# Local attention and whitening on one core: VectorE's order in image 0 written out, evictions and the first softmax put first

## The chip, the cores and the metric

The kernel runs on one core of a Trainium2 chip. Five engines work side by side, each through its own queue of instructions in order: TensorE (PE in the profile, its weight loads PEld), VectorE (DVE), ScalarE (ACT), GpSimd (POOL) and SyncE (SP), which issues most of the DMA transfers. Instructions of different engines wait for each other by semaphores. The metric is the device time of one execution in microseconds. Before the change the median of three runs was 827.57 us (821.6 to 827.88).

## What is computed

The input x has 4 images of 256 channels and 64 by 64 pixels. Layer 0 computes 49 attention logits for each pixel by a 7 by 7 convolution with dilation 2 to 128 channels and a 1 by 1 convolution to 49; a softmax over the 49; and the sum of the 49 shifted copies of x with these weights. Layer 1 whitens groups of 64 channels: mean and covariance over all images and pixels, five Newton steps for the inverse square root, and a linear map of every pixel.

```python
k = conv(x, w1, padding=6, dilation=2) + b1      # 128 channels
k = conv1x1(k, w2) + b2                          # 49 channels
attn = softmax(k, axis=1)
y = einsum('bkchw,bkhw->bchw', shifts_of_x, attn)
# layer 1: groups of 64 channels, all pixels of all images
Sigma = EPS * I + cov(y);  P = I
for _ in range(5):
    P = 1.5 * P - 0.5 * P @ P @ P @ (Sigma / trace)
out = (P * sqrt(1 / trace)) @ (y - mean) * weight + bias
```

## The kernel before

**Weights.** The two convolutions have no nonlinearity between them, so the kernel first multiplies the filters (lines 204 to 235): the result is the tile `tap`, 49 logits for each of 7 by 7 taps and 256 channels. `cv_buf` is a pair of PSUM tiles used here first and by the convolution later.

**The convolution by interpolation.** Logits are computed as in a Winograd scheme: polynomials in the row direction and in the column direction are evaluated at 7 points (0, 1, -1, 2, -2, a sixth point and infinity; `EVAL`, `INF`), multiplied, and interpolated back. For one row point `br` this takes: `row_weights` (line 307, sums of taps, into `gbr` or `gb5`, with scratch in `lgx`), `weights` (line 342, the column sums for a bank of column points, into the tiles `wr`, one buffer for each of the three banks), `row_eval` (line 412, sums of the image's rows, into `rb`), `col_eval` (line 443, sums of columns, into the tiles `xh`), `conv_bank` (line 471, the matmuls, into one of the two `cv_buf` tiles, and an eviction by ScalarE into `pv`), and `col_interp` (line 544, 22 small VectorE operations, into `zz`). A row point has three banks of column points, `BANKS`, of 96, 80 and 32 matmuls. VectorE does all sums; it is the busiest engine after TensorE. For each operation of this kind the helper `in_turn` (line 266) can tie the order: while `strict` is set, each such operation is made to follow the one before it.

**Image 0 is different.** Only three of its row points (1, 2, 3) go through the banks. The others (0, 4, 5 and infinity) are computed by `direct` (line 582): 56 matmuls over 7 column taps each, straight from the rows. `direct0` (line 670) lets them write the PSUM tile `acc`, which has two halves; infinity takes the second half, row 0 the first and, later, the second. The result goes to `zz` or `zi` by a ScalarE eviction (line 607), or (line 609 and the next) by a small ScalarE copy and a VectorE addition. `keep_weights` scales the weights of rows 4 and 5 and stores them to DRAM for the images after. Then `row_interp` interpolates over the row points, in two parts, and writes the logits `lg`, for image 0 in the memory of `store[4]`; ScalarE adds the bias (line 578).

**Softmax and weighted sum.** `softmax(b, pc)` (line 742) transposes the logits of one column parity on TensorE into two of the three `tp` buffers, takes the maxima (`mx`) on VectorE, 16 exponentials on ScalarE (`d`), and normalises on VectorE. `move_terms` (line 785) copies the weights with ScalarE into `zt` in skewed form, 16 copies for each of four quarters `n` of an image, and stores `zt` to DRAM (`sd`). `load_band` loads it back shifted, and VectorE transposes it in place (line 852); then the tile `band` is a banded matrix. `make_block` turns pixels by TensorE and evicts them to `xb`; `weighted_sum` multiplies `xb` with `band` into `y`; `store_y` evicts it over the memory of x; `turn_y` turns y again, evicts to `yt`, and `moments` adds to the covariance. The end of the kernel whitens.

**What sets the order.** TensorE's matmuls keep the order of the program (`keep_in_program_order`). On the other engines a scheduler chooses among the ready instructions by priority, so VectorE's and ScalarE's orders come from it, apart from what `in_turn` ties. The loop at line 1079 runs the rows of images 1 to 3 bank by bank, each step with a cost, and spreads over them (`gap`, `todo`) the softmax and the eight half-steps of the image before: `plan` gives each piece one of eight places in an image. In image 1 the direct convolution for infinity (`direct_inf`) follows the first row's three banks; the two softmaxes of image 0 stand at places 0 and 1.

These lines show how the first two direct convolutions stand ahead of the conv steps, and how infinity shares the tile:

```python
direct(0, br, sr, acc[:, 1 if br == INF else sr], w)
...
direct0(INF, 0)
direct0(0, 0)
for k in range(NR0):
    ...
    for i in range(len(BANKS)):
        conv_step(k, i)
```

Of the kernel before, what the change touches and what calls it, by code (L numbers as in the profile page):

```python
# [2 lines left out]

# [20 lines left out]
INF = 6  # L24
# [7 lines left out]
def kernel(  # L32
# [246 lines left out]

    @contextmanager  # L280
    def in_order():
        strict[0] = True
        yield
        strict[0] = False

    def add(o, a, b):
        return in_turn(TT(o, a, b, ALU.add))  # L287
# [54 lines left out]
    def weights(b, br, i):  # L342
# [15 lines left out]
        if br == 0:  # L358
            g = [gr0[:, v] for v in range(KS)]
        elif br in kept:  # L360

            f = rb[0].rearrange("p q r c w -> p (q r c w)")[:, : KS * NSK]
            if i == 0:
                nc.sync.dma_start(f, kept[br])
            f = f.rearrange("p (v a r k) -> p v a r k", v=KS, a=NCC, r=2)
            g = [f[:, v] for v in range(KS)]
        else:
            if i == 0:
                row_weights(br)
            g = [gbr[:, v] for v in range(KS)]  # L370
        g = [t.rearrange("p a r k -> p (a r k)") for t in g]
        e, o, e1 = (
# [98 lines left out]
    def conv_bank(b, br, i, w):  # L471

        if i == 0:
            pvs[b, br] = apool.tile(
                [P, NP, Q9, 2 * Q9], F32, tag="pv", name=f"pv_{b}_{br}", bufs=2
            )
        pts = BANKS[i]
        i0 = sum(len(k) for k in BANKS[:i])
        cv = cv_buf[ncv[0] % 2][:, : 3 * PT].rearrange(
            "p (n q b two) -> p n q b two", n=3, two=2, b=Q9  # L480
        )
        ncv[0] += 1
        for k, bc in enumerate(pts):
            terms = [(sr, sc, cc) for sc in taps(bc) for sr in taps(br) for cc in range(NCC)]
            wv = w[bc].rearrange("p c (a r k) -> p c r a k", r=len(taps(br)), a=NCC)
            for j, (sr, sc, cc) in enumerate(terms):

                n = Q9 if j == 0 and bc == INF else Q8
                for h in range(2):
                    pe(  # L490
                        nc.tensor.matmul(  # L491
                            cv[h * HB : h * HB + KT, k, sr : sr + n, sc : sc + n],
                            wv[:, sc, sr, cc],
                            xh[bc][:, :n, h * NCC + cc, :n],
                            start=(j == 0),
                            stop=(j == len(terms) - 1),
                            skip_group_check=True,
                        )
                    )
        nc.scalar.copy(  # L500
            pvs[b, br][:K2, i0 : i0 + len(pts)].rearrange("p n q b -> p (n q b)"),
            cv[:K2, : len(pts)].rearrange("p n q b two -> p (n q b two)"),
        )

    def interpolate(pt, tmp, outs, cut, part=None):

# [75 lines left out]
    def direct(b, br, s, ps, w, xr=None):  # L582
# [21 lines left out]
                )  # L604
        z = zi[b % 2][:K2] if br == INF else zz[:K2, br]
        if s == 0:
            nc.scalar.copy(z[:, :Q8], ps[:K2])  # L607
        else:
            nc.scalar.copy(z[:, Q8], ps[:K2, Q8 - 1])
            add(z[:, 1:Q8], z[:, 1:Q8], ps[:K2, : Q8 - 1])  # L610

    gi = dram.tile([P, KS, NCC * KT], F32, name="gi")
    nc.sync.dma_start(gi, tap[:, UPOS[3]].rearrange("p v a k -> p v (a k)"))

    def direct_inf(b):

        t = apool.tile([P, KS, NCC, KT], F32, tag="wi", name=f"wi_{b}")
        nc.sync.dma_start(t.rearrange("p v a k -> p (v a k)"), gi.rearrange("p v k -> p (v k)"))
        w = [t[:, v] for v in range(KS)]
        ps = cv_buf[ncv[0] % 2].rearrange("p (q w) -> p q w", w=W)  # L620
        ncv[0] += 1
        direct(b, INF, 0, ps, w)

    acc = ps_y.tile([P, 2, Q8, W], F32, tag="y", name="acc")
    nc.vector.memset(acc, 0.0)
# [11 lines left out]
        nxt.update(w)  # L637
        col_eval(cur["x"], i)

    for i in range(len(BANKS)):  # L640
        prepare(0, i)

    def conv_step(k, i):
        w = {bc: nxt.pop(bc) for bc in BANKS[i]}
        b, br = rows[k]
# [2 lines left out]
        if end:  # L648

            with in_order():  # L650
                if i == len(BANKS) - 2:
                    col_interp(b, br, 0)
                elif i == len(BANKS) - 1:
                    col_interp(b, br, 1)
                    row_interp(b, 1)
        if k + 1 < len(rows) and k != NR0 - 1:
            prepare(k + 1, i)
        if i == len(BANKS) - 1 and not end:
            if b > 0 and br == ROWS[-2]:
# [10 lines left out]
    def direct0(br, sr):  # L670
# [3 lines left out]
        else:  # L674
            u = KS - 1 - 4 * sr - (3 if br == INF else 0)
            w = [tap[:, UPOS[u], v] for v in range(KS)]
            direct(0, br, sr, acc[:, 1 if br == INF else sr], w)

    direct0(INF, 0)
    direct0(0, 0)  # L680
    for k in range(NR0):
        if k == NR0 - 1:
            row_weights(4)
            keep_weights(4)
            xrs[4] = row_eval(0, 4)
        for i in range(len(BANKS)):
            conv_step(k, i)
        if k == 1:
            direct0(0, 1)
            for s in range(2, 4):  # L690
                load_x(s, s, nc.gpsimd)
    row_weights(5)
    keep_weights(5)
    xrs[5] = store[4].rearrange("p c r w -> p (c r w)")[:, SH * W :].rearrange(
        "p (q r c w) -> p q r c w", q=Q8, r=2, c=NCC
    )
    row_eval(0, 5, [rb[0], rb[1], xrs[5]])

    for sr in range(2):
        nc.scalar.copy(  # L700
            gr0[:, :, :, sr].rearrange("p v a k -> p (v a) k"),
            tap[:, UPOS[KS - 1 - 4 * sr]].rearrange("p v a k -> p (v a) k"),
        )
    direct0(4, 0)
    with in_order():
        direct0(4, 1)
        row_interp(0, 0)
    direct0(5, 0)
    for i in range(len(BANKS)):
        prepare(NR0, i)  # L710
    with in_order():
        direct0(5, 1)
        row_interp(0, 1)
    gpool.release()

    npix = SH * W // 4
    nc.vector.tensor_reduce(
        pivot, slots[0].rearrange("p a r w -> p a (r w)")[:, :, :npix], AX.X, ALU.add  # L720
    )
    nc.vector.tensor_scalar(pivot, pivot, -1.0 / npix, None, ALU.mult)

# [61 lines left out]
    def move_terms(n):  # L785
# [7 lines left out]
        for j in range(CR):  # L793
            for u in range(CR):
# [8 lines left out]
                    offset=o[:, e].offset,  # L803
                    ap=[list(o.ap[0]), [KS * SW, NCH], [(KS - CR) * SW, ne], [1, KS]],
                )
                if k % 2 == 0 or b < B - 1:
                    nc.scalar.copy(o, i)  # L807
                else:
                    nc.vector.tensor_copy(o, i)
                k += 1  # L810
        nc.sync.dma_start(
            sd[n % 2].rearrange("(p f) -> p f", p=P),
# [22 lines left out]
    def load_band(n, part):  # L835
# [13 lines left out]
                ),  # L849
            )  # L850
        f = band[:, m0:m1].rearrange("p m r w -> p (m r w)")
        nc.vector.transpose(f, f)  # L852
        if n > 4 * (B - 1):
            bring_back(dma)

# [8 lines left out]
    def make_block(n, m):  # L864
# [9 lines left out]
                )  # L874
            )
        xb = bpool.tile([P, C], F32, tag="xb", name=f"xb_{n}_{m}", bufs=4)
        (nc.vector.tensor_copy if tail else nc.scalar.copy)(xb, t[:, :C])  # L877
        blocks[n, m] = xb


# [27 lines left out]
    def store_y(n, half):  # L908
        yt, pc = where(n)
        ps = y_ps.pop((n, half))  # L910
        for cc in range(NCC):
            o = yt[:, cc, half * HALF : (half + 1) * HALF, bass.ds(pc, SW, 2)]
            if tail and cc:
                nc.vector.tensor_scalar(o, ps[:, cc], pivot[:, cc : cc + 1], None, ALU.add)
            else:
                nc.scalar.activation(o, ps[:, cc], AF.Identity, bias=pivot[:, cc : cc + 1])  # L916

    count = [0]
    ybs = {}
# [1 line left out]
    def turn_y(n, i):  # L921
        yt, pc = where(n)
        t = tp()
        for cc in range(NCC):
# [5 lines left out]
                )  # L930
            )
        yb = ybs[n, i] = yt_buf[i % NY]
        nc.scalar.copy(  # L933
            yb.rearrange("p a g c -> p (a g) c")[:, :, :GW],
            t[:, :C].rearrange("p (e c) -> p e c", c=GW),
        )

    def moments(n, half):

# [108 lines left out]
        todo.setdefault((b + j // NPC, j % NPC), []).extend(what)  # L1048

    def soft(b, pc):  # L1050
        softmax(b, pc)
        soft_done.add((b, pc))
        bands(4 * b + pc)

# [13 lines left out]
            for j in range(8):  # L1068
                plan(b + 1, 3 + j, hs[j])
    for b in range(B):  # L1070
        for j in range(2):
            plan(b + 1, j, lambda b=b, j=j: soft(b, j))
    plan(1, 2, lambda: load_x(4, 4, nc.gpsimd))

# [4 lines left out]
    for b in range(1, B):  # L1079

        steps = []
        for r in range(len(ROWS)):
            k = NR0 + len(ROWS) * (b - 1) + r
            for i, cost in enumerate((6, 5, 2)):
                steps.append((cost, lambda k=k, i=i: conv_step(k, i)))

        steps.insert(len(BANKS) if b == 1 else 0, (12, lambda b=b: direct_inf(b)))
        j, at, whole = 0, 0, sum(c for c, _ in steps)
        for cost, f in steps:
            f()  # L1090
# [169 lines left out]
```

## Time and profile before

The span of the profiled execution is 824.6 us, that of its run 826.37 us.

| stretch, us | PE busy | VectorE busy | ScalarE busy |
|---|---|---|---|
| 0 to 40 | 28.16 | 18.77 | 10.53 |
| 40 to 80 | 27.21 | 40.00 | 7.64 |
| 80 to 120 | 38.86 | 39.93 | 15.01 |
| 120 to 160 | 36.22 | 22.19 | 7.81 |
| 160 to 200 | 39.16 | 38.76 | 12.72 |
| 200 to 220 | 10.81 | 16.80 | 14.95 |
| 220 to 300 | 75.19 | 61.12 | 38.09 |
| 300 to 340 | 36.63 | 38.55 | 16.81 |

Each row is the busy time of an engine in that stretch, so a row is read against its length. Image 0's convolution lies between 33 and 170 us, image 1's begins at 170, the first softmax is at 181 to 215, and the first weighted sum at 216. From 220 on TensorE is busy nearly all the time up to the whitening at 750. The later lines of the profile are read in the same way: start and duration in us, engine and line, what is written from what, and, in brackets, how long the engine sat idle ahead of it and what ended the wait.

### The profile page before, as it was taken

What the parts mean: (1) busy time and instruction counts of PE and PEld (TensorE: products, weight loads), DVE (VectorE), ACT (ScalarE), POOL (GpSimd) and SP (SyncE); (2) the same over time, 40 slices, a digit from 0 to 9 for tenths busy, and PEclk for the clock granted to TensorE, in tenths of its full rate; (3) what the DMA queues carried; (4) which work ended last, traced back from release to release, by engine and by line L of the source; (5) the groups of instructions that cost most, each with busy time, mean ns of one, the idle gap of its engine ahead of it and who ended that gap; (6) DMA issues with size and microseconds to landing.
All of it is one profiled execution on the core that took longest, in us unless ns stands there. A gap on an engine that the chain in (4) does not pass through costs nothing.

```text
span 824.6 us, 18450 instructions
## 1 busy us (share of the span) xinstructions
PE 733.9 (89%) x7444; PEld 550.4 (67%) x7444; DVE 620.4 (75%) x1314; ACT 346.2 (42%) x1018; POOL 34.0 (4%) x46
## 2 busy tenths in 40 slices
PE   5839999899589989988999999889999789888997
PEld 1416762276469877777899948778897668675443
DVE  2799992999697979988986999498979654444443
ACT  1321440126654524468433435665334563322443
POOL 0310000030000010001000100000000000000000
PEclk9979999999789999999999999899999999899999
DMA  8990210043534472066445621442421137810576
GB/s 332 206 315 20 76 70 1 30 150 114 163 118 153 169 236 70 19 221 228 145 120 188 196 57 31 125 169 74 156 66 38 46 118 242 243 46 2 229 305 281
DMA packets 60013, 114.76 MB, mean 139 GB/s; under 512 B 22759, under 2 KB 41880, under 8 KB 59032
## 3 DMA queue, kind: packets, MB, share of 16 engines
q1 hardware_dynamic: 56232, 94.71, 35.3%
q0 software_dynamic: 3696, 18.88, 6.8%
q8 instruction: 59, 0.97, 0.5%
q14 instruction: 26, 0.21, 0.1%
HBM read 66.23 MB, written 47.33 MB: 138 GB/s over the span
## 4 chain that ended last, share of the span: by engine, by line
PE 45%; DVE 31%; ACT 13%; DMA 6%; issue 4%; SPq 0%; DVEq 0%; ACTq 0%
PE y L898 13%; PE cv L491 7%; ACT zt L807 7%; PE tp L1206 7%; PE acc L596 4%; DMA sd<-zt 3%; DVE xh L294 3%; PE tp L870 3%; PE sig L946 3%; PE tp L926 3%; DVE zz L294 2%; ACT d L766 2%; DVE pv L294 2%; DVE rb L287 2%; DVE band L852 2%
## 5 line engine op out<-in xcount | busy, mean ns | idle before, releaser
L491 PE MATMUL cv<-xh,wr 128*49 128x128 f32 x4368 | 250.1, 275 | 5.0 <-DVE pv L290 3.6
L491 PEld LDWEIGHTS cv<-xh,wr 128*49 128x49 f32 x4368 | 243.6, 124 | 9.8 <-ACT zt L807 3.8
L898 PE MATMUL y<-band,xb 128*128 128x224 f32 (+2 forms) x640 | 167.0, 404 | 21.3 <-DVE band L852 12.5
L898 PEld LDWEIGHTS y<-band,xb 128*128 128x128 f32 x640 | 119.2, 209 | 48.5 <-issue 18.2
L807 ACT COPY zt<-d 32x112 f32<-32x112 f32 x224 | 62.8, 281 | 21.6 <-DMA sd<-zt 15.6
L870 PE MATMUL tp<-ident,slot 128*128 128x128 f32 x256 | 51.8, 305 | 19.0 <-ACT yt L933 13.9
L916 ACT ACTIVATE slot<-y,pivot 128x512 f32<-128x512 f32 x53 | 36.7, 738 | 72.7 <-PE y L898 72.7
L933 ACT COPY yt<-tp 128x256 f32<-128x256 f32 x128 | 44.8, 376 | 45.7 <-PE tp L926 44.4
L926 PE MATMUL tp<-ident,slot 128*128 128x128 f32 x256 | 53.6, 306 | 7.9 <-ACT yt L933 2.7
L870 PEld LDWEIGHTS tp<-ident,slot 128*128 128x128 f32 x256 | 40.3, 206 | 27.0 <-ACT yt L933 15.9
L852 DVE STREAM_TRANSPOSE band<-band 128x960 f32<-128x960 f32 (+1 forms) x48 | 50.6, 1058 | 10.0 <-DMA band<-sd 9.9
L500 ACT COPY pv<-cv 113x486 f32<-113x486 f32 (+1 forms) x63 | 30.1, 477 | 60.4 <-PE cv L491 60.2
L926 PEld LDWEIGHTS tp<-ident,slot 128*128 128x128 f32 x256 | 41.6, 206 | 19.1 <-issue 5.0
L596 PE MATMUL acc<-slot,tap 128*49 128x480 f32 (+3 forms) x168 | 37.1, 588 | 14.0 <-ACT zi L607 12.8
L1221 DVE TENSOR_SCALAR out<-tp,scale,beta 128x512 f32<-128x512 f32 x32 | 25.9, 810 | 29.5 <-PE tp L1206 29.5
L766 ACT ACTIVATE d<-tp,mx 128x49 f32<-128x49 f32 x128 | 36.4, 340 | 18.1 <-issue 9.1
L877 ACT COPY xb<-tp 128x256 f32<-128x256 f32 x87 | 30.4, 375 | 19.2 <-PE tp L870 17.9
L1217 ACT ACTIVATE out<-tp,beta,scale 128x512 f32<-128x512 f32 x32 | 24.9, 778 | 32.0 <-PE tp L1206 32.0
L294 DVE SCALAR_TENSOR_TENSOR xh<-ct 128x512 f32<-128x512 f32 x42 | 27.6, 684 | 13.9 <-PE cv L491 13.9
L596 PEld LDWEIGHTS acc<-slot,tap 128*49 128x49 f32 x168 | 11.8, 127 | 37.9 <-issue 22.1
L946 PE MATMUL sig<-yt 128*64 128x65 f32 x1024 | 36.9, 225 | 0.0
L946 PEld LDWEIGHTS sig<-yt 128*64 128x64 f32 x1024 | 32.4, 137 | 6.0 <-issue 4.5
(202 smaller groups left out, 1005.8 us busy)
## 6 DMA issues: line engine op xcount, KB each, us to landing
out_dram<-out SPq DMA_DIRECT2D x32, 512.0 KB, 2.6
sd<-zt SPq DMA_DIRECT2D x16, 896.0 KB, 4.4
slot<-in_x_dram POOLq DMA_DIRECT2D x12, 1024.0 KB, 9.7
band<-sd SPq DMA_DIRECT2D x128, 84.0 KB, 2.1
wr<-gd SPq DMA_DIRECT2D x15, 588.0 KB, 4.1
wr<-gd SPq DMA_DIRECT2D x15, 490.0 KB, 3.4
w<-in_L_conv_w_dram SPq DMA_DIRECT2D x4, 1568.0 KB, 11.3
spill<-slot POOLq DMA_DIRECT2D x3, 2048.0 KB, 7.8
```

The lines of the kernel that those rows point to most:

```text
L294: return in_turn(STT(o, a, f, b, ALU.mult, ALU.add))
L491: nc.tensor.matmul(cv[h * HB : h * HB + KT, k, sr : sr + n, sc : sc + n], wv[:, sc, sr, cc], xh[bc][:, :n, h * NCC + cc, :n], start=(j == ...
L596: nc.tensor.matmul(ps[h * HB : h * HB + KT, :, w0:w1_], w[v][:, cc], xs[:, :, cc, w0 + d : w1_ + d], start=(j == 0), stop=(j == len(order) ...
L766: nc.scalar.activation(d[:, h, i], lt[i // NI][:, i % NI, h, :KT], AF.Exp, bias=mx[:, i, h : h + 1], accum_out=s[:, h, i : i + 1],)
L807: nc.scalar.copy(o, i)
L852: nc.vector.transpose(f, f)
L870: nc.tensor.transpose(t[:, cc * P : (cc + 1) * P], xt[:, cc, CR * m : CR * (m + 1), bass.ds(pc, SW, 2)], ident,)
L898: nc.tensor.matmul(ps[:, cc, q0 - half * HALF : q1 - half * HALF, :], xb[:, cc * P : (cc + 1) * P], rhs, start=(k == 0), stop=(k == len(PI ...
L926: nc.tensor.transpose(t[:, cc * P : (cc + 1) * P], yt[:, cc, CR * i : CR * (i + 1), bass.ds(pc, SW, 2)], ident,)
L933: nc.scalar.copy(yb.rearrange("p a g c -> p (a g) c")[:, :, :GW], t[:, :C].rearrange("p (e c) -> p e c", c=GW),)
L946: nc.tensor.matmul(sig[g * GW : (g + 1) * GW, cc], yb[:, cc, g, :GW], yb[:, cc, g], start=(count[0] == 0 and cc == 0), stop=(count[0] == 4 ...
L1206: nc.tensor.matmul(t, wm[cc], slots[2 * b + pr][:, cc, q * TR : (q + 1) * TR, :].rearrange("p r w -> p (r w)"), start=True, stop=True,)
```

## The change

VectorE's operations of image 0 are written out in one fixed order (`strict` stays set from the first to the last of them), and the calls stand in that order: the first row's weights and inputs, the infinity and row 0 sums, the weights of rows 2 and 5 and row 2's input before the first bank, and so on. `conv_step` is no longer used for image 0. Infinity of image 0 goes to a `cv_buf` tile (`conv_psum`) instead of a half of `acc`. Top priority (`tc.high_priority()`) is given to the evictions of the conv banks, of direct convolutions, of `xb`, of `y` and of `yt`, to the chains in `in_order`, to the band transposes, to the zt copies of an image's first quarter, and to each image's first softmax. The two softmaxes of image 0 stand ahead of and behind the third bank of image 1's first row, ahead of `direct_inf`; before they came after that bank, and after `direct_inf`. It is meant to have VectorE do first what the next matmuls wait for, and to have no eviction or softmax stand behind other work.

```diff
     def in_order():
+        was = strict[0]
         strict[0] = True
-        yield
-        strict[0] = False
+        with tc.high_priority():
+            yield
+        strict[0] = was
...
-            if i == 0:
-                row_weights(br)
             g = [gbr[:, v] for v in range(KS)]
...
-        nc.scalar.copy(
-            pvs[b, br][:K2, i0 : i0 + len(pts)].rearrange("p n q b -> p (n q b)"),
...
+        with tc.high_priority():
+            nc.scalar.copy(
+                pvs[b, br][:K2, i0 : i0 + len(pts)].rearrange("p n q b -> p (n q b)"),
...
         if s == 0:
-            nc.scalar.copy(z[:, :Q8], ps[:K2])
+            with tc.high_priority():
+                nc.scalar.copy(z[:, :Q8], ps[:K2])
...
+    def conv_psum():
+        ncv[0] += 1
+        return cv_buf[(ncv[0] - 1) % 2].rearrange("p (q w) -> p q w", w=W)
...
-            direct(0, br, sr, acc[:, 1 if br == INF else sr], w)
-
+            direct(0, br, sr, conv_psum() if br == INF else acc[:, sr], w)
+
+    def bank(k, i):
+        conv_bank(0, rows[k][1], i, {bc: nxt.pop(bc) for bc in BANKS[i]})
...
+    strict[0] = True
+    three = range(len(BANKS))
+    row_weights(1)
+    for i in three:
+        nxt.update(weights(0, 1, i))
+    xr = row_eval(0, 1)
+    for i in three:
+        col_eval(xr, i)
     direct0(INF, 0)
     direct0(0, 0)
-    for k in range(NR0):
-        if k == NR0 - 1:
-            row_weights(4)
-            keep_weights(4)
-            xrs[4] = row_eval(0, 4)
-        for i in range(len(BANKS)):
-            conv_step(k, i)
-        if k == 1:
-            direct0(0, 1)
-            for s in range(2, 4):
-                load_x(s, s, nc.gpsimd)
+    row_weights(2)
+    xr = row_eval(0, 2)
     row_weights(5)
     keep_weights(5)
...
+    for i in three:
+        bank(0, i)
+        nxt.update(weights(0, 2, i))
+        col_eval(xr, i)
+    for s in range(2, 4):
+        load_x(s, s, nc.gpsimd)
+    for i in three:
+        bank(1, i)
+    col_interp(0, 1)
+    row_weights(3)
+    xr = row_eval(0, 3)
+    for i in three:
+        nxt.update(weights(0, 3, i))
+        col_eval(xr, i)
+        if i == 0:
+            direct0(0, 1)
+    for i in three:
+        bank(2, i)
+    row_weights(4)
+    keep_weights(4)
+    xrs[4] = row_eval(0, 4)
+    col_interp(0, 2)
...
+    row_eval(0, 5, [rb[0], rb[1], xrs[5]])
+    col_interp(0, 3)
     direct0(4, 0)
-    with in_order():
-        direct0(4, 1)
-        row_interp(0, 0)
+    direct0(4, 1)
+    row_interp(0, 0)
     direct0(5, 0)
-    for i in range(len(BANKS)):
+    for i in three:
         prepare(NR0, i)
-    with in_order():
-        direct0(5, 1)
-        row_interp(0, 1)
+    direct0(5, 1)
+    row_interp(0, 1)
+    strict[0] = False
...
+                with tc.high_priority() if n % 4 == 0 else nullcontext():
+                    if k % 2 == 0 or b < B - 1:
+                        nc.scalar.copy(o, i)
...
-        nc.vector.transpose(f, f)
+        with tc.high_priority():
+            nc.vector.transpose(f, f)
...
     def soft(b, pc):
-        softmax(b, pc)
+        with tc.high_priority() if pc == 0 else nullcontext():
+            softmax(b, pc)
...
-        steps.insert(len(BANKS) if b == 1 else 0, (12, lambda b=b: direct_inf(b)))
+        inf = (12, lambda b=b: direct_inf(b))
+        if b == 1:
+
+            steps[:3] = [
+                *steps[:2], (0, lambda: soft(0, 0)), steps[2], (0, lambda: soft(0, 1)), inf,
+            ]
+        else:
+            steps.insert(0, inf)
```

The evictions of `xb`, `y` and `yt` are wrapped in the same way as that of `pv`, and the reduction for `pivot` is tied behind the last operation of the written order.

## The prediction

> **What bounds the kernel now.** I read the page first: busy shares, slices, the chain that ended last. TensorE (PE) is busy 89% of the span and VectorE (DVE) 75%. In the slices PE stays at 8 or 9 from the fourth to the thirty-first, except in the eleventh (5); it is low in the first and the third.
>
> ```profile
> PE 733.9 (89%) x7444; PEld 550.4 (67%) x7444; DVE 620.4 (75%) x1314; ACT 346.2 (42%) x1018; POOL 34.0 (4%) x46
> PE   5839999899589989988999999889999789888997
> DVE  2799992999697979988986999498979654444443
> ```
>
> So what can be won is PE's idle time, and the two large pieces of it lie where the change works. The timeline of PE (start, duration, what, and in brackets the idle time ahead and who ended it) shows them:
>
> ```profile
> 36.01 10.72 PE L596 MATMUL acc<-slot,tap 128*49 128x512 f32 x50 [1.22 <-DMA slot<-in_x_dram]
> 59.52 12.90 PE L596 MATMUL acc<-slot,tap 128*49 128x512 f32 x56 [12.79 <-ACT zi L607]
> 72.26 23.34 PE L491 MATMUL cv<-xh,wr 128*49 128x128 f32 x416
> 95.44 11.54 PE L596 MATMUL acc<-slot,tap 128*49 128x512 f32 x56
> ...
> 119.93 11.59 PE L596 MATMUL acc<-rb,gbr 128*49 128x512 f32 x56 [0.17 <-DVE rb L294]
> ...
> 169.87 11.76 PE L491 MATMUL cv<-xh,wr 128*49 128x128 f32 x208
> 181.56 1.22 PE L752 MATMUL tp<-ident,slot 113*128 113x113 f32 x8
> 182.71 11.59 PE L596 MATMUL cv<-slot,wi 128*49 128x512 f32 x56
> ...
> 216.34 2.47 PE L898 MATMUL y<-band,xb 128*128 128x320 f32 x4 [9.19 <-DVE band L852]
> ```
>
> PE idles 12.79 us before 59.52 and 9.19 us before the first weighted sum at 216.34; after that its waits are of 0.4 to 3.6 us. The ScalarE (ACT) timeline tells why:
>
> ```profile
> 58.05 0.95 ACT L408 ACTIVATE wr<-wr 128x392 f32<-128x392 f32 x2 [4.50 <-DVE wr L294]
> 58.91 0.56 ACT L607 COPY zi<-acc 113x512 f32<-113x512 f32 x1
> ...
> 192.23 0.30 ACT L766 ACTIVATE d<-tp,mx 128x49 f32<-128x49 f32 x1 [9.14 <-issue]
> ...
> 198.19 4.63 ACT L807 COPY zt<-d 32x112 f32<-32x112 f32 x16 [0.62 <-DVE d L779]
> ```
>
> The infinity sums were complete at 46.7, but their eviction stands behind two weight scalings that wait for DVE, and starts at 58.91; the next direct convolution writes the same tile acc and waits. The first exponentials wait for the maxima, which DVE takes late:
>
> ```profile
> 174.65 4.62 DVE L287 TENSOR_TENSOR rb<-slot 128x1024 f32<-128x1024 f32 x4
> ...
> 189.72 0.69 DVE L294 SCALAR_TENSOR_TENSOR xh<-xh,rb 128x512 f32<-128x512 f32 x1
> 190.32 0.32 DVE L287 TENSOR_TENSOR ct<-pv 113x162 f32<-113x162 f32 x1
> 190.56 0.56 DVE L758 TENSOR_REDUCE mx<-tp 128x8 f32<-128x392 f32 x1
> ```
>
> **What the Trainium skill says.** "PSUM — Partial Sum Buffer", section "Engine vs sequencer instructions": ScalarE's and VectorE's queues are strict FIFO. The trace agrees: the eviction ready at 46.7 runs at 58.91. "TensorE: Matmul & The Clock Gate", section "What's actually happening": the array's clock is gated down after about 3.4 us without work and released after as much busy time. The trace fits: the 56 matmuls after the 12.79 us gap take 12.90 us, the same 56 take 11.54 at 95.44; 1.36 us more.
>
> **The change, part by part.** Prices are start-to-start distances in the DVE timeline: a 196-element operation 0.27 us, 686 elements 0.785, 512 elements 0.60, 1024 elements 1.14, 2048 elements 2.2, interpolation steps 0.24 (22 make one column interpolation, 5.2), row interpolation steps 0.79. PE: a direct convolution 11.6, a row of conv banks 11.67 for 208 matmuls (5.4, 4.5, 1.8 by bank).
>
> *1. Infinity into a conv bank.* The direct convolution of row 0 no longer shares a tile with an eviction: it starts at 46.7, and at 11.6 to 12.9 ends near 58.9 (before 72.2). The eviction has until the second conv bank needs that buffer, near 64; its new place on ACT, after two xh copies, gives about 49.5.
>
> *2. DVE's order in image 0.* Step by step from the end of the last shared operation, 35.35: 20 weight operations 5.4 (40.8), row evaluation 4×1.14+2.2 (47.6), column evaluation 6.5 (54.1; bank 0's inputs are there at 50, so PE doesn't wait at 58.9). Then gbr 1.6, rb 2.2, row 5's weights 6×0.785: 62.6. The next weights overwrite the buffer that bank 0 reads until 64.3: a wait of about 1.3 us that the trace of before does not show; behind it stand all of DVE's later steps. Row 2's inputs follow at 68.1, 72.4 and 75.8; PE needs them from 70.6, and runs on to 82.3. Then interpolation 5.2 (81.0), weights 3.9, rows 7.0 (91.9), bank weights 1.9 and columns 2.3: row 3's first inputs at 96.2. PE meanwhile does the direct convolution 0,1 (82.3 to 93.9), waits 2.3, and ends row 3 at 107.9. Before: 119.8. Row 4's sums 1.6+2.2 follow by 108.2, the scaled weights by 108.0: start near 108.3 instead of 119.93. The four direct convolutions to 170.05 keep their 50 us less about 0.7 (the eviction before the last one, which waited 2.12, is now placed between the bias steps): image 1's first bank at about 157.9 instead of 169.87. The other DVE work there (17.6 us of interpolation and row 5) lies before 132, in a stretch where before DVE sat idle 16.15 us. **Won so far: 12.0 us.**
>
> *3. First softmax earlier.* In the new order two conv banks (9.9), 8 transposes (1.2), the third bank (1.8), 4 transposes of the second softmax (0.7) come before image 1's infinity. PE is through at 171.4. DVE ends the logits at 162.4, then pivot 1.1, four rb 4.7, one rb 2.2, and only then two maxima: 171.5, negated after one more ct: 172.7. Exponentials 172.9 to 177.5. The second softmax's other 4 transposes need a tp buffer (there are three) that the twelfth exponential frees, at 172.9+12×0.277=176.2; in the trace of before the same distance is 192.23 to 195.79. **New PE wait: 176.3−171.4=4.9 us**, with infinity and everything later queued behind. Infinity to 188.6, two banks to 198.5. The path to the band: column steps and scaling to 178.2, zt 4.65 (182.9), then as before 12.2 us from zt's end at 202.82 to the transpose at 215.07, and 1.1: band at 196.2. So PE no longer waits for it. But ACT's order now holds the first three zt copies of the third band ahead of the first xb: they wait for the store of the second band (second exponentials to 187.5, its zt to 194.7, store 4.9): 199.8, then 0.9, a bank eviction 0.6, two xb 0.7. First weighted sum near 202.0 instead of 216.34. Inside that half the other zt copies stand ahead of xb twice, 1.2 us each, so it ends near 210.3 where before it ended at 223.2. **Won: 12.9.** The third band's zt is then done at 208 rather than at 230, so the wait of 3.23 at 240.33 (yt behind zt copies of the fourth band) and of 0.45 after it fall away: **3.7 more, 16.6.**
>
> *4. Top priority for evictions, chains and bands.* PE's order from the first weighted sum on is unchanged. Nearly all of ACT's and DVE's later instructions stay within five places of where they were; yt copies move up by 4 places once and by 5 to 20 in the last image, against its waits (2.62, 1.01, 2.45 us at 654 to 668, behind exponentials). Between 0 and 4 us; I take 1. The band transposes that move up in images 2 and 3, and the rows delayed by a few places at 530 to 560, I cost at nothing: the conv bank at 547 waited for an operation (3.58 us) that stands only one place later. The nullcontext, wrapped code and helper for the buffer move no instruction.
>
> Sum: 12.0+0.9+3.7+1=17.6; 827.6−17.6=**810.0 us**.
>
> **Rivals.** *Weaker:* the waits in part 3 are worse (zt copies waiting for stores, the second softmax): first weighted sum at 206 and the 3.23 stays, so 12.0−3+0=9: 818. For: those copies are strictly ahead on ACT. Against: stores took 4.5 to 4.9 here. *Stronger:* evictions first removes half of the 25 us of small PE waits between 236 and 640 as well: 798. Against: ACT's order hardly changes there. *No change:* the lead is eaten by the next bound: DVE is busy 38.55 of 40 us in 300 to 340, so PE could catch up with it and wait: 825. Against: DVE idles about 19 us between 216 and 300, waiting for PE, and its own start comes 12 us earlier. *Slower:* prioritised work delays xh copies and column steps in the 18 rows of images 1 to 3; 1.9 us a row costs 34 and leaves 827.6−17.6+34=844. Against: those rows' order moves by single places, 0.24 to 0.7 us each.
>
> **Numbers.** Forecast 0.56, weaker 0.15, stronger 0.14, no change 0.09, slower 0.06. The first falls to 803 to 817; the range, 800 to 822, takes in the unknown sizes (tp wait 3.3 to 7, first half 1 to 4, the last image 0 to 4) and most of the weaker case. One per cent is 819.3: faster 0.80 (first, stronger, most of weaker), same 0.13, slower 0.07.
>
> **What would show it.** No gap before the second direct convolution, PE without a wait until a short one before row 3; image 1's first bank near 158; a new wait of about 5 us in the second softmax's transposes; first weighted sum near 202, ended by ACT and not by the band; no 3 us wait in the first second half. Wrong if DVE's written-out order waits longer for a buffer than 1.3 us, if DVE's load after 300 takes the lead back, or if weight loads from DRAM come late.

## The result, and the profile after

The changed kernel takes 802.54 us against 827.63 us (the median of before with a fourth run), a ratio of 0.9705 with a 95% interval of 0.9653 to 0.9756. It is 7.5 us faster than forecast. The span of its profiled execution is 801.0 us (before 824.6).

These are the page's busy line and the slices of TensorE (PE) and VectorE (DVE):

```profile
PE 725.7 (91%) x7444; PEld 547.5 (68%) x7444; DVE 626.9 (78%) x1314; ACT 345.6 (43%) x1018; POOL 34.2 (4%) x46
PE   5899789997999999988999999978999899798997
DVE  2699998999798999977996997696979665435443
```

The low third slice of PE (3 before) is gone, but new dents (7) stand in the fifth, the tenth and the twenty-seventh. DVE is 6.5 us busier with the same 1314 instructions, which nothing in the diff asks for: a first sign that they overlap less. PE is 8.2 us less busy (733.9 before) with the same 7444 matmuls: they run faster, and the part on the priorities shows where. PE's timeline shows where the dents are (start, duration, what, idle time ahead):

```profile
36.37 11.61 PE L597 MATMUL cv<-slot,tap 128*49 128x512 f32 x48 [2.07 <-DMA slot<-in_x_dram]
...
48.60 10.76 PE L597 MATMUL acc<-slot,tap 128*49 128x512 f32 x52
...
59.97 23.04 PE L491 MATMUL cv<-xh,wr 128*49 128x128 f32 x409
...
101.69 13.18 PE L491 MATMUL cv<-xh,wr 128*49 128x128 f32 x208 [6.96 <-DVE xh L289]
...
115.54 11.59 PE L597 MATMUL acc<-rb,gbr 128*49 128x512 f32 x56 [0.66 <-DVE rb L296]
...
164.86 9.98 PE L491 MATMUL cv<-xh,wr 128*49 128x128 f32 x176
...
184.69 1.03 PE L780 MATMUL tp<-ident,slot 113*128 113x113 f32 x4 [6.12 <-DVE ct L296]
185.65 13.70 PE L597 MATMUL cv<-slot,wi 128*49 128x512 f32 x56
```

The 12.79 us before the second direct convolution are gone, and rows 1 and 2 run without a gap. But row 3 waits 6.96 us for its inputs, and the second softmax's transposes 6.12 (for a `tp` buffer, which the twelfth exponential frees at 184.65). On ScalarE (ACT) both evictions that stood behind other work now come early:

```profile
49.89 0.59 ACT L609 COPY zi<-cv 113x512 f32<-113x512 f32 x1
...
181.14 0.30 ACT L794 ACTIVATE d<-tp,mx 128x49 f32<-128x49 f32 x1 [0.76 <-DVE mx L789]
```

Infinity is evicted at 49.89 (before 58.91), and the first exponential starts at 181.14 (before 192.23).

To see where time was won I compare, at places that every kernel passes, the start of the same matmuls before and after. The later places are the starts of the moments' sums (sig), named by their time in the kernel before.

| place, time before | lead forecast, us | lead measured, us |
|---|---|---|
| image 1's first bank, 169.87 | 12.0 | 5.0 |
| first weighted sum, 216.34 | 14.3 | 6.2 |
| sums at 247 | 16.6 | 12.2 |
| sums at 322 | – | 16.9 |
| sums at 412 | – | 19.1 |
| sums at 566 | – | 16.6 |
| end of the last image, 749 | 17.6 | 24.6 |

The forecast won too much in image 0 and too little after 247.

Two cautions on such leads. The first sums of image 0 on DVE start at 29.54 before and at 29.05 after (29.6 to 30.3 in the experiments), since loads arrive differently from run to run; a difference of 1 us between two traces can be no more than that. And between 389 and 412 every trace gains 2.9 to 3.5 us, also the one whose only change is infinity's tile: there the trace of before has a wait of 1.67 us and twelve slow weighted sums behind it (4.77 us against 3.18). So about 3 us of the lead from 412 on can't be credited to the order or to the priorities.

### The profile page after: what moved, and what is told of

Same layout as the page of the kernel before. It is cut to its first block, busy times and chain, and to the rows that moved or that the text cites. A ratio compares the mean times of both kernels' runs of the same rounds, so it can differ in the third digit from the quotient of the medians.

```text
span 801.0 us, 18449 instructions
## 1 busy us (share of the span) xinstructions
PE 725.7 (91%) x7444; PEld 547.5 (68%) x7444; DVE 626.9 (78%) x1314; ACT 345.6 (43%) x1018; POOL 34.2 (4%) x46
## 4 chain that ended last, share of the span: by engine, by line
PE 40%; DVE 28%; ACT 11%; DMA 5%; issue 3%; SPq 0%; DVEq 0%; ACTq 0%
PE y L930 11%; PE cv L491 9%; PE tp L1247 7%; ACT zt L837 6%; DVE xh L296 4%; DMA sd<-zt 3%; PE acc L597 3%; PE sig L980 3%; PE tp L901 3%; PE tp L959 2%; DVE band L883 2%; DVE zz L296 2%; DVE rb L296 2%; ACT d L794 2%; DVE pv L296 2%
## 5 line engine op out<-in xcount | busy, mean ns | idle before, releaser
L930 PE MATMUL y<-band,xb 128*128 128x224 f32 (+2 forms) x640 | 158.6, 387 | 17.0 <-ACT xb L909 8.9
L930 PEld LDWEIGHTS y<-band,xb 128*128 128x128 f32 x640 | 113.2, 199 | 42.0 <-ACT xb L909 12.5
L837 ACT COPY zt<-d 32x112 f32<-32x112 f32 (+1 forms) x224 | 62.9, 281 | 24.6 <-DMA sd<-zt 18.2
L901 PE MATMUL tp<-ident,slot 128*128 128x128 f32 x256 | 50.6, 300 | 16.6 <-ACT yt L967 16.6
L949 ACT ACTIVATE slot<-y,pivot 128x512 f32<-128x512 f32 x53 | 36.5, 736 | 60.0 <-PE y L930 59.9
L959 PE MATMUL tp<-ident,slot 128*128 128x128 f32 x256 | 52.3, 300 | 4.0 <-ACT xb L909 1.2
L959 PEld LDWEIGHTS tp<-ident,slot 128*128 128x128 f32 x256 | 41.4, 205 | 14.3 <-issue 4.4
L794 ACT ACTIVATE d<-tp,mx 128x49 f32<-128x49 f32 x128 | 36.7, 329 | 11.6 <-DVE mx L789 11.5
L296 DVE SCALAR_TENSOR_TENSOR xh<-ct 128x512 f32<-128x512 f32 x42 | 28.0, 688 | 12.2 <-PE cv L491 12.0
L597 PE MATMUL cv<-slot,wi 128*49 128x496 f32 (+3 forms) x168 | 36.9, 598 | 0.0
L1247 PE MATMUL tp<-slot,PS 128*128 128x512 f32 x80 | 35.9, 593 | 0.0
L909 ACT COPY xb<-tp 128x256 f32<-128x256 f32 x87 | 30.5, 375 | 11.7 <-PE tp L901 10.7
```

Source lines behind the costliest of these rows:

```text
L296: return in_turn(STT(o, a, f, b, ALU.mult, ALU.add))
L597: nc.tensor.matmul(ps[h * HB : h * HB + KT, :, w0:w1_], w[v][:, cc], xs[:, :, cc, w0 + d : w1_ + d], start=(j == 0), stop=(j == len(order) ...
L794: nc.scalar.activation(d[:, h, i], lt[i // NI][:, i % NI, h, :KT], AF.Exp, bias=mx[:, i, h : h + 1], accum_out=s[:, h, i : i + 1],)
L901: nc.tensor.transpose(t[:, cc * P : (cc + 1) * P], xt[:, cc, CR * m : CR * (m + 1), bass.ds(pc, SW, 2)], ident,)
L930: nc.tensor.matmul(ps[:, cc, q0 - half * HALF : q1 - half * HALF, :], xb[:, cc * P : (cc + 1) * P], rhs, start=(k == 0), stop=(k == len(PI ...
L959: nc.tensor.transpose(t[:, cc * P : (cc + 1) * P], yt[:, cc, CR * i : CR * (i + 1), bass.ds(pc, SW, 2)], ident,)
```

## The experiments

Two questions follow. Why did image 0 give 5 us and not 12? One theory: DVE's written order puts each operation directly behind the one whose result it reads, and that costs more than the prices I took from the interleaved order of before. Its rival: DVE waits for buffers that PE frees, and the operations cost the same. And who won the 12 us after 247: the priorities, or the head start of image 0 passing through? Each ratio below is to the kernel before as it ran beside that experiment, at 825.9 to 826.5 us.

**Infinity's tile by itself.** The kernel before with this alone:

```diff
-            direct(0, br, sr, acc[:, 1 if br == INF else sr], w)
+            direct(0, br, sr, conv_psum() if br == INF else acc[:, sr], w)
```

> The kernel before with one edit: infinity of image 0 goes to a conv bank. Theory A (VectorE bounds image 0's convolution): the 12.79 us gap of PE goes, but PE then waits for VectorE further on, VectorE's sums for row 4 still end near 119.8 us, the first direct convolution of row 4 still starts near 120, and the time stays within 3 us of the kernel before, 825 to 828. Theory B (PE's wait for the tile acc was itself the cost): row 4 starts near 108, image 1's first bank near 158, and the time falls by 10 to 12 us, to about 816.

Measured: 825.18 us, ratio 0.9987 (0.9971 to 1.0003): no gain, as the first theory said. The gap of 12.79 us before the direct convolution is gone, and PE's timeline shows the same gap further down:

```profile
82.19 13.20 PE L491 MATMUL cv<-xh,wr 128*49 128x128 f32 x208 [12.21 <-DVE xh L287]
```

Image 1's first bank starts at 169.91, as before. So the eviction held PE at one place, while DVE's inputs set the end of that stretch. The inverse, the changed kernel with infinity back in `acc`:

```diff
-            direct(0, br, sr, conv_psum() if br == INF else acc[:, sr], w)
+            direct(0, br, sr, acc[:, 1 if br == INF else sr], w)
```

> The changed kernel with one edit undone: infinity of image 0 goes to acc again. The second direct convolution then waits for the eviction at 49.9, so it starts about 3 us later. Theory A (VectorE bounds): the wait of 6.96 us before row 3 shrinks by those 3 us, image 1's first bank stays at 165, time within 2 us of the changed kernel's 802.5. Theory B: everything moves by 3 us and the time is 805 to 806.

Measured: 805.58 us, ratio 0.9733 (0.9695 to 0.9772). The time's interval overlaps that of the changed kernel, but the trace agrees with the second theory: PE waits 4.21 us for `zi` before 51.18, row 3 starts at 105.62 (101.69 in the changed kernel) with a wait of still 6.80 us, and image 1's first bank at 168.78 (164.86). DVE has become later as well: at 69.69 it waits 3.47 us for PE to free the buffer of row 1's weights, a wait that the changed kernel doesn't have. So DVE is tied to PE as soon as PE is late. With the written order, the tile is worth 3 us (the medians) to 4 us (these places), without it nothing.

**What an operation costs directly behind one that it depends on.** These are 162-element steps of a column interpolation. Before, the scheduler placed weight operations and steps that don't depend on each other one behind the other; after, the steps stand as they are written (start, duration):

```profile
92.88 0.32 DVE L294 SCALAR_TENSOR_TENSOR pv<-ct,pv 113x162 f32<-113x162 f32 x1
93.12 0.32 DVE L287 TENSOR_TENSOR pv<-pv 113x162 f32<-113x162 f32 x1
93.36 0.32 DVE L290 TENSOR_TENSOR pv<-pv 113x162 f32<-113x162 f32 x1
```

```profile
79.87 0.33 DVE L289 TENSOR_TENSOR pv<-pv 113x162 f32<-113x162 f32 x1
80.23 0.33 DVE L292 TENSOR_TENSOR pv<-pv 113x162 f32<-113x162 f32 x1
80.60 0.33 DVE L289 TENSOR_TENSOR pv<-pv 113x162 f32<-113x162 f32 x1
...
81.56 0.33 DVE L296 SCALAR_TENSOR_TENSOR ct<-ct,pv 113x162 f32<-113x162 f32 x1
81.93 0.33 DVE L296 SCALAR_TENSOR_TENSOR ct<-pv,ct 113x162 f32<-113x162 f32 x1
```

The durations are equal, the distance of the starts is 0.24 us before and 0.36 to 0.37 after: before, the next operation starts while the last is still running; after, it doesn't. The program says how these depend on each other. The one at 81.93 reads what the one at 81.56 wrote. The first three read no result of the one ahead: the one at 80.23 overwrites `s4`, which the one at 79.87 reads, and the one at 80.60 overwrites `s3`. Both kinds wait, in the trace, for a semaphore that DVE's own operation ahead raises.

All of DVE's steps from 35.25 to 101.46, where row 3's first inputs start, can be sorted in this way. Of 117, 63 don't depend on the one directly ahead, and each of them keeps the prediction's price within 0.02 us. The other 54, of which 45 read its result and nine only overwrite what it reads, are each 0.11 us or more longer, 7.1 us in all.

To price this alone, one kernel runs nothing but such operations.

```python
for k in range(24): op(chain[:, 0], chain[:, 0], n)           # reads the one directly ahead
for k in range(24): op(pair[:, k % 2], pair[:, k % 2], n)     # reads the one before that
for k in range(24): op(free[:, k % 4], c[:, n : 2 * n], n)    # reads no result
```

> All of the reference's computation is left out; only VectorE operations run: 24 of a kind in a row, for 162, 196, 512 and 1024 elements, as a chain in which each reads the result of the one directly ahead, as two chains in alternation, and as operations that read no result at all. Theory A: a chain costs about 0.12 us more for each operation than the other two (0.36 against 0.24 us for 162 elements, 1.26 against 1.14 for 1024). Theory B: all three cost the same, and what made the written order longer was something else.

DVE's timeline, for 162 and for 1024 elements:

```profile
5.96 8.66 DVE L68 TENSOR_TENSOR chain<-chain,c 128x162 f32<-128x162 f32 x24 [3.90 <-DMA c<-in_x_dram]
14.54 5.78 DVE L68 TENSOR_TENSOR pair<-pair,c 128x162 f32<-128x162 f32 x24
20.24 5.78 DVE L68 TENSOR_TENSOR free<-c 128x162 f32<-128x162 f32 x24
...
195.88 30.10 DVE L68 TENSOR_TENSOR chain<-chain,c 128x1024 f32<-128x1024 f32 x24
225.90 27.33 DVE L68 TENSOR_TENSOR pair<-pair,c 128x1024 f32<-128x1024 f32 x24
253.15 27.33 DVE L68 TENSOR_TENSOR free<-c 128x1024 f32<-128x1024 f32 x24
```

From start to start, a chain takes (14.54−5.96)/24=0.358 us an operation and the pair (20.24−14.54)/24=0.238: 0.12 us more. At 1024 elements it is 30.02/24=1.251 against 27.25/24=1.135: again 0.12. 196 and 512 elements give 0.389 against 0.273 and 0.718 against 0.602, and multiply-adds the same. The price is a fixed one for each operation that depends on its neighbour; one operation between is enough to avoid it. This chain also overwrites what the operation ahead reads, so it is the kernel's trace that shows that either is enough. Whether the time goes into the dependence or into the semaphore by which the program expresses it, no run here separates.

What it is worth in the kernel: the changed kernel with the same operations moved apart, wherever their order is written out, for instance

```diff
             add(E, T[6], T[4])
             add(O, T[5], T[3])
-            add(S0, E, O)
             add(E1, T[2], T[0])
+            add(S0, E, O)
             add(S1, E1, T[1])
```

and likewise in `weights`, in row 5 of `row_eval` and in `interpolate`.

> The changed kernel with VectorE's same operations of image 0 in another written order inside the helpers: operations that need the result of the one directly ahead are moved apart where another is free. Theory A (in the written order each operation that reads the result of the one directly ahead starts 0.12 us later, and some 40 of these ahead of row 3 made VectorE 5 us late): PE's wait before row 3 falls from 6.96 to 1 to 3 us, image 1's first bank comes at 159 to 161, time 795 to 798. Theory B (the lateness comes from something else, such as waits for buffers): wait and time unchanged, 801 to 804.

Measured: 793.18 us, ratio 0.959 (0.9556 to 0.9624), faster than either theory said. The 54 operations have become 26. Row 3 starts at 98.90; counted from DVE's first sum of image 0, so that late loads drop out, at 68.60 us instead of 72.64, 4.0 earlier. This is the best reproduced number here: the two later kernels with image 0 moved apart and the order otherwise as written give 68.64 and 68.62, and of three others with image 0 as in the changed kernel two give 72.67 and 72.63, the third 73.41, of which 0.96 is a wait for a buffer that PE frees late. PE's wait there is still 5.97 us, since PE reaches the place 1.8 us earlier in that run, and not under 3 as the first theory said. To see where the 9 us come from, the moving apart was done in image 0 alone, and in the chains of images 1 to 3 alone, by a flag that is set in one part:

```diff
-        for k in other if strict[0] else range(len(ops)):
+        for k in other if strict[0] and weave[0] else range(len(ops)):
```

> The changed kernel with dependent VectorE operations moved apart in image 0 only; the chains of images 1 to 3 stay as they are in the changed kernel. Theory A: most of the 9 us that moving them apart everywhere won comes through image 0's 3 to 4 us head start and what follows from it (the shorter wait near 533): 794 to 796. Theory B: the head start is all that image 0 gives, and the rest is won in the chains of images 1 to 3: 798 to 800.

Measured: 797.77 us, ratio 0.9668 (0.9648 to 0.9688), between the two theories and nearer the second. Row 3 starts 3.1 us earlier than in the changed kernel (98.58), image 1's first bank 2.7, the first weighted sum 4.3, and from 247 to the end the distance stays at 4.3 to 4.7 us: as the second theory says, image 0 gives its head start and no more.

> The changed kernel with dependent operations moved apart only in the chains of images 1 to 3; image 0 as in the changed kernel. Theory A: what moving apart wins in image 0 (4.4 us) and later (about 4.6) add up: 797 to 799, with the same milestones as the changed kernel until 450 us. Theory B: the later part works only on top of a head start from image 0: 801 to 803.

Measured: 798.48 us, ratio 0.9654 (0.9615 to 0.9692). Until 449 this kernel is 0.4 to 1.5 us behind the changed one, and its image 0 starts 1.1 us later; then, up to 566, it gains 5, and ends 4.0 ahead. In the medians 4.8 us (image 0) and 4.1 (later) stand against 9.4 for both together, so they add up, as the first theory said.

**The priorities.** The changed kernel without any:

```diff
-        with tc.high_priority():
+        with nullcontext():
```

> The changed kernel with every top priority taken out. Theory A: the written order and infinity's bank give what was won up to 220 us (about 6 us at the first weighted sum), but the priorities are what removes the waits behind exponentials in the last image and the yt wait near 240: the lead stops at 10 to 12 us and the time is 810 to 815. Theory B: the priorities hardly move an instruction, and the later lead comes from running ahead of VectorE and the DMA: 801 to 805.

Measured: 813.5 us, ratio 0.9862 (0.9839 to 0.9885), as the first theory said. And the kernel before with the priorities alone, everything else as it was:

> The kernel before, with the top priorities alone; VectorE's order of image 0, infinity's tile and the places of the softmaxes are as before. Theory A: image 1's first bank stays at 170 and the first weighted sum at 214 to 216; what is won is the last image's waits and half of the middle, 7 to 10 us: 817 to 821. Theory B: priorities are worth nothing without the order, since the chains are scheduled as before: 825 to 828.

Measured: 806.92 us, ratio 0.9779 (0.9754 to 0.9803), far below either expectation. The leads over the kernel before, at the places of the table:

| place | changed kernel | no priorities | priorities alone |
|---|---|---|---|
| 169.87 | 5.0 | 3.8 | 0.0 |
| 216.34 | 6.2 | 4.4 | 3.7 |
| 247 | 12.2 | 11.4 | 4.7 |
| 322 | 16.9 | 11.9 | 9.8 |
| 412 | 19.1 | 14.9 | 12.0 |
| 566 | 16.6 | 15.1 | 11.7 |
| 749 | 24.6 | 15.2 | 18.0 |

The kernel without priorities holds the written order, infinity's tile and the new places of the softmaxes, of which the order and the places were not run apart from each other. These together bring most of what is won up to 247, and keep it. The priorities bring 4 to 5 us between 247 and 322, and 6 to 8 in the last image; without them the last image gains nothing. There the kernel without priorities shows the same two waits of PE behind exponentials as the kernel before, of 2.62 and 2.45 us; this is the first:

```profile
639.25 0.50 PE L901 MATMUL tp<-ident,slot 128*128 128x128 f32 x2 [2.62 <-ACT d L794]
```

In the changed kernel ACT puts the `yt` copy among the exponentials instead of behind all sixteen:

```profile
633.00 0.32 ACT L794 ACTIVATE d<-tp,mx 128x49 f32<-128x49 f32 x1
...
633.27 0.39 ACT L967 COPY yt<-tp 128x256 f32<-128x256 f32 x1
...
633.52 0.34 ACT L794 ACTIVATE d<-tp,mx 128x49 f32<-128x49 f32 x1
```

These waits are short, and what they cost is more than their length. In the last image (635 to 749, the same 803 or 804 matmuls in each trace):

| kernel | length, us | PE busy, us | granted clock |
|---|---|---|---|
| before | 114.3 | 97.7 | 0.94 |
| changed, no priorities | 114.2 | 97.7 | 0.94 |
| before, priorities alone | 107.6 | 93.9 | 0.98 |
| changed | 105.9 | 92.2 | 1.00 |

Of the 8.4 us that the changed kernel wins there, PE's idle time gives 2.9; the other 5.5 are the same matmuls run faster: the clock was granted at half for 13.7 us before, and is not once now. A sum of waits alone would price the priorities at a third of what they bring here.

15.2 and 18.0 are more than 24.6 together: part of each gain is won by either alone, such as the first weighted sum's 9.19 us for the band. Priority alone brings that sum forward by 3.7 us, and the changed kernel without priorities by 4.4. The priorities also cost something: in both kernels that have them, and not in the other two, whose longest wait there is 3.6 to 3.7 us, PE waits 7.57 to 7.78 us near 543. ACT's timeline of the changed kernel shows on what:

```profile
536.19 0.61 ACT L837 COPY zt<-d 32x112 f32<-32x112 f32 x2 [4.01 <-DMA sd<-zt]
...
537.51 2.72 ACT L837 COPY zt<-d 32x112 f32<-32x112 f32 x9
...
540.60 1.44 ACT L837 COPY zt<-d 32x56 f32<-32x56 f32 x5
...
542.53 0.66 ACT L967 COPY yt<-tp 128x256 f32<-128x256 f32 x2
```

The zt copies of a band that nobody needs yet wait 4.01 us for the store of the one before, and `yt`, which PE waits for, stands behind them.

**Where the second softmax stands.** The changed kernel with it behind infinity:

```diff
-                *steps[:2], (0, lambda: soft(0, 0)), steps[2], (0, lambda: soft(0, 1)), inf,
+                *steps[:2], (0, lambda: soft(0, 0)), steps[2], inf, (0, lambda: soft(0, 1)),
```

> The changed kernel with image 0's second softmax behind the direct convolution for infinity instead of ahead of it. Theory A (PE's 6.12 us wait for a tp buffer, and the 13.7 us that infinity then takes instead of 11.6, are on the path): no wait at the second softmax, first weighted sum at 202 to 204 instead of 210.1, time 795 to 798. Theory B (the band of the first quarter, or the zt copies ahead of xb, would end the wait anyway): first weighted sum within 2 us of 210, time 801 to 805.

Measured: 801.38 us, ratio 0.9697 (0.9666 to 0.9729), as the changed kernel. The wait of 6.12 us is gone and infinity takes 11.55 us instead of 13.70, but, as the second theory said, the first weighted sum starts at 208.77 against 210.14:

```profile
208.77 2.50 PE L930 MATMUL y<-band,xb 128*128 128x320 f32 x4 [6.08 <-ACT xb L909]
```

The wait moved. ACT's `xb` copies at 208.34 stand behind three zt copies of a later band, which start at 206.96 after 3.58 us in which ACT idles, for a reason that the profile doesn't name.

**Two faster versions.** With operations moved apart, each zt copy is tied behind the last eviction of `y` that precedes it in the program:

```diff
-                        nc.scalar.copy(o, i)
+                        ins = nc.scalar.copy(o, i)
+                        if evicted[0] is not None:
+                            tc.add_manual_dep(ins.ins, evicted[0], ...)
```

> Dependent operations moved apart everywhere, and each zt copy tied behind the last eviction of y that precedes it in the program, so that no zt copy that waits for a store stands ahead of xb or yt on ScalarE. Theory A: ScalarE's order is what holds TensorE at 208 and at 533 (waits of about 6 us each and smaller ones at 338 and 365); both go, and the time is 782 to 788. Theory B: the wait only moves to the band, which comes that much later: 791 to 796, with waits for the band in place of those for xb and yt.

Measured: 786.37 us, ratio 0.9527 (0.9502 to 0.9552), as the first theory said. The wait near 533 is gone, and between 527 and 566 the lead grows from 26.5 to 33.2 us (with operations moved apart alone it fell from 28.5 to 27.1). It costs 1.4 to 2.4 us between 286 and 364, won back by 389, and 2.0 at 527.

Last, row 1's interpolation, 22 operations ahead of row 3's inputs, is moved behind row 4's sums; row 3's bank results go to free space in the logits' tile, so that they need not wait for it:

```diff
-    col_interp(0, 1)
     row_weights(3)
...
     xrs[4] = row_eval(0, 4)
+    col_interp(0, 1)
     col_interp(0, 2)
```

> The kernel with operations moved apart and zt copies tied, and row 1's column interpolation (22 VectorE operations) moved behind row 4's sums; row 3's bank results go to free space of the logits' tile, so that they don't wait for it. Theory A: the wait of 6 us before row 3 is VectorE's work that stands ahead of its inputs: it falls to under 1 us, image 1's first bank comes near 157, and the time is 780 to 783. Theory B: something else (PE's release of row 2's inputs, the scaling on ScalarE) holds row 3: the wait stays over 3 us, and the time is 785 to 788.

Measured: 781.3 us, ratio 0.9457 (0.9407 to 0.9507), the fastest, and as the first theory said. PE's timeline has no wait before row 3, and image 1's first bank starts at 157.39:

```profile
92.63 12.05 PE L517 MATMUL cv<-xh,wr 128*49 128x128 f32 x208
...
157.39 9.99 PE L517 MATMUL cv<-xh,wr 128*49 128x128 f32 x176
```

So the work that stood ahead of row 3's inputs on DVE was the wait there. A smaller one has come up behind it: PE waits 2.66 us for DVE's `zz` before 132.71, where it had none over 2 us. The ratio's interval just touches that of the step before; the milestones give 5.4 us.

## Why the prediction was right, and where it was not

*What bounds the kernel.* Right: the two gaps of PE at 59.52 and 216.34 were what could be won first. Incomplete: as much was won after 247 (12.4 us) as up to it (12.2), though no wait over 3.6 us stood there.

*Step 1, infinity.* Right in detail: the direct convolution runs from about 48 to 59.9 without a gap (forecast 46.7 to 58.9), the eviction is at 49.89 (forecast 49.5). The first experiment adds that the step alone is worth nothing.

*Step 2, DVE's order.* The mechanism was right, PE waits for row 3's first inputs; the term "row 3's first inputs at 96.2, PE waits 2.3" was mis-sized: they came near 101.7, and PE waited 6.96. What failed is the list of prices: they were read in the timeline of before, where unrelated work stands between dependent operations. The buffer wait of 1.3 us did not come: DVE is late, PE has freed the buffer, and the 0.20 us at this place end with DVE's own `ct`.

```profile
65.76 0.36 DVE L289 TENSOR_TENSOR wr<-ct 128x196 f32<-128x196 f32 x1 [0.20 <-DVE ct L289]
```

So DVE's operations alone took between 6 and 7 us more than forecast, and the 7.1 us of the 54 operations that depend on the one directly ahead account for all of it; moving 28 of them apart gained back 4.0. Behind row 3 the loss persisted: 5.0 us won at image 1 where 12.0 stood.

*Step 3, the first softmax.* The new wait was there, as forecast: 6.12 us against 4.9. Its other cost was not forecast: infinity behind it takes 13.70 us instead of 11.6, although the prediction had read the same effect behind the gap at 59.52. The 7 us of step 2 shifted everything. The zt copies ahead of the first `xb` wait for a store as forecast (2.30 us, to 208.29), but PE is itself busy with the banks until then and waits only 0.30 us before the first weighted sum at 210.14. The end of that half was summed wrongly: 202.0, the 6.9 us of before and twice 1.2 give 211.3, not 210.3. That the waits of 3.23 and 0.45 us after 240 fall away was right. From the first weighted sum to 247 the lead grew by 6.0 us where 2.3 were forecast, in good part because the twelve weighted sums behind those waits run faster (3.18 us against 5.46 at half the clock).

*Step 4, the priorities.* "Between 0 and 4 us; I take 1" was the largest error of size: taking them away costs 9.4 us at the end of the last image. I had compared the places of instructions, found most within five places, and costed that at nearly nothing. But sixteen exponentials, 0.28 us from start to start, are 4.4 us of queue; what counts is how long the work takes that stands between, not how many places it is. And I had counted the waits of the last image by their length, without the slow matmuls behind them, which were worth more. The 7.57 us wait near 543 is a cost of theirs that I missed.

That the sum came near is luck: two errors offset each other, 4.4 us too much up to 247 and 11.4 too little after it; 11.4−4.4=7.0, against 7.5 measured. Of the rivals, *stronger* (798) came nearer than the forecast, but not for its reason: between 247 and 635 PE's small waits sum to 22.7 us before and 22.4 after, as the wait near 543 takes the place of those that went; after 247 they fell in the last image alone. *No change* and *slower* did not happen: DVE's load in 300 to 340 took nothing back.

## What to carry to other kernels

Take an operation's price from a stretch where it has the neighbours that it will have; where an order is written out by hand, put something between an operation and one that reads its result or overwrites its input. Price a wait of TensorE with the slow matmuls behind it, not by its length. Judge a change of an in-order queue by what stands ahead of the instruction that the bounding engine waits for, in microseconds, and look above all for early work that waits for a transfer: it holds up everything behind it. A gap that one edit removes can stand somewhere else an instant later, so follow a fixed set of places through the whole span.

## What the hardware showed

- A VectorE operation that depends on the one directly ahead starts 0.12 us later than one that doesn't (0.358 against 0.238 us for 162 elements, 1.251 against 1.135 for 1024), and not only when it reads the result: nine that merely overwrite what the one ahead reads pay it as well. The Trainium skill, "VectorE: DVE Perf Modes", section "The DRAIN you can't avoid", says that the next operation starts when the pipeline is empty, that one which isn't held starts earlier, and that leaving out semaphores didn't make a row of copies faster. The timeline here agrees that there are two cases: independent operations of 0.32 us start 0.24 us apart, so that they overlap, and only those that depend on their neighbour pay the full length. No run here leaves the semaphores out.
- PE behind an idle stretch is slower for a while: 56 matmuls of infinity take 11.55 to 11.58 us in four traces without a wait ahead, and 12.59 to 13.85 in eight with one of 4.96 to 6.72. In the changed kernel the granted clock is 0.50 from 183.2 to 189.8, around the wait of 6.12. This agrees with the Trainium skill, "TensorE: Matmul & The Clock Gate", section "What's actually happening", as the prediction cites it; a wait of 5 to 7 us costs another 1.0 to 2.3. It does not take 3.4 us without any work: in the trace of before, PE is busy for 1.68 of the 3.4 us from 403.6 to 407.0, with one wait of 1.67 in it, and the clock is granted at 0.50 from 407.0 to 410.4.
